# Turning rows by VectorE and DMA instead of TensorE in a four-layer block, and moving DMA issues from SyncE to ScalarE

## The chip, the cores and the metric

The kernel runs on one core of one Trainium2 chip. The metric is the device time of one launch in microseconds (us), as the median of several runs. The engines are named as in the profile: PE (TensorE, with its weight loads PEld), DVE (VectorE), ACT (ScalarE), POOL (GpSimd) and SP (SyncE, which only issues DMAs here). Each engine works through its own list of instructions in order and waits at semaphores for the others.

## The reference

Four layers follow each other on an input of 4 batches of 512 rows with 512 features, each with a layer norm in front and a residual sum behind:

```python
x = x + attn_a(layernorm(x), Wq, Wk, Wv, Wo)      # 16 heads, 4 key heads, width 128
x = x + ffn(layernorm(x), w1, w2, w3)              # ternary weights, width 1408
x = x + attn_b(layernorm(x), wq, wk, wv, wo, ...)  # 16 heads, block-scaled weights
x = x + ffn(layernorm(x), w1, w2, w3)              # the same weights again
```

Attention a is the mean of two: softmax attention of rotated queries and keys under a causal mask, and a gated linear attention, whose state decays at each row by `exp(log_sigmoid(k) / 16)`; there queries and keys are softmaxed over the 128 features instead of rotated. The feed-forward layer is `(sigmoid(x1) * x2) @ w3q.T` with `x1 = x @ w1q.T`, `x2 = x @ w2q.T` and weights rounded to -1, 0, 1.

## The kernel before, in words

All arithmetic of the main path is in 32-bit floats. Where the weights are exact in fewer bits, an operand is split into a high and a low half ("xnhi", "xnlo"), and two matmuls of a faster kind take the place of one. PE contracts over partitions, so rows have to be turned (transposed) before they are multiplied.

**Layer norm.** `layernorm_steps` (L123) gives the normalised rows of one batch in four chunks of 128. Each chunk takes statistics (L132, L133), a scale (L138 to L145), the normalised chunk `xn` (L160), four PE transposes of 128x128 into a bank of PSUM (L165), and the evacuation: a copy on ACT in attention, and in the feed-forward a split into halves by ACT and DVE (L120, L121). It is a generator: its user calls for the next part between other work.

**First attention** (`first_attention_gentle`). A group is one batch and one key head with its four query heads; there are 16 groups of four chunks, so 64 chunks. `Group` projects keys and values (L188 through `project`), makes the gates and the decays (`decays`): the running decay `down`, its value at each chunk's last row (`ends`, three small DMAs by SP, L420), its inverse `held`, the rotated keys `kr` (two DVE operations, L343 and L346, and two on POOL between them, L345), and the softmaxed, decayed keys `kd` (L358). `transposes` turns `kr` and `kd` by PE, four transposes each (L364); ACT evacuates them, with a factor 1/sqrt(128) for `krT` (L430). `states` (L439 to L443) follows.

`Chunk` has the parts A (project 128 query rows of four heads), B (softmaxed, decayed queries `qd` and rotated queries `qr`), L, C (PE turns `qr`), own (scores of the linear attention inside the chunk, L480), D(h) (for one head: scores by PE L490, mask and maximum by DVE L494, exponential by ACT L497, reciprocal L498, division by ACT L499, a turn of 32x32 blocks by DVE L500), E, F (L515 to L522: the product with the values) and G (the output projection and the residual sum, L193).

Queries `qd` and weights `pr` are turned without PE already: DVE turns 32x32 blocks, SP stores the tile to DRAM (`queries` L463, `passed` L503), and four DMAs of 32 partitions each read it back with the blocks in their places (L, L470, and E, L509).

**Order.** `step(n)` runs one part of several chunks: E and own for chunk n, D for n+1, C and L for n+2, A and B for n+3, F for n-1, G for n-2, and between them parts of the next group (`part(m, p, half)`: projections for p = 0 and 1, decays at p = 2, transposes at p = 3, states at p = 4), of a layer norm (`ln`) and of the quantisation of the feed-forward weights (`quant`, which loads a block by SP and takes its absolute sum by ACT, L233). For steps 0 to 63 PE's instructions stand in the order of the program (`manual_schedule`); on the other engines a scheduler places them when it expects their inputs, but instructions under `in_place` keep the program's order among themselves.

**Second feed-forward layer** (`feed_forward` with `last`). For each batch 11 blocks of 128 hidden features: two times eight matmuls (L188), then sigmoid on ACT (L1097), product on DVE (L1098), split into halves; then for each chunk of rows 22 matmuls and the residual sum (L1109), and the store of the output (L1111). The normalised rows of the next batch are made meanwhile by `halved`, one call behind each block from the third on (two behind the third).

Of the kernel before, what the change touches and what calls it, by code (L numbers as in the profile page):

```python
# [19 lines left out]
P = 128  # L20
# [54 lines left out]
def hybrid_block(ctx: ExitStack, tc: tile.TileContext, a: dict, out: bass.AP):  # L75
# [47 lines left out]
    def layernorm_steps(b, sink, tag="tp", apart=False, place=lambda i: i):  # L123

# [21 lines left out]

        if not apart:
            for c in range(NC):
                moments(c)
                if c == 1:  # L150
                    yield
            scales(slice(0, NC))
        for c in range(NC):
            if apart:
                moments(c)
                scales(slice(c, c + 1))
            else:
                yield
            xn = lnp.tile([P, C], F32, tag="xn", name="xn", bufs=1)
            nc.vector.tensor_scalar(xn, xs[b * NC + c], mv[:, c, 0:1], rstd[:, c : c + 1], ALU.subtract, ALU.mult)  # L160
            if not apart:
                yield
            tp = bank(tag, [P, NK, P])
            for k in range(NK):
                t = nc.tensor.transpose(tp[:, k, :], xn[:, k * P : (k + 1) * P], ident)  # L165
                if k == 0:
                    place(t)
            sink(c, tp)
# [5 lines left out]
    def halved(pool, b, **kw):  # L174

        halves = [pool.tile([P, NK, S], F32R, tag=f"xn{n}", name=f"xn{n}") for n in ("hi", "lo")]
        return halves, layernorm_steps(b, lambda c, tp: split(*(h[:, :, c * P : (c + 1) * P] for h in halves), tp), **kw)

# [132 lines left out]
    def first_attention_gentle(base, extra):  # L311
# [6 lines left out]
        with ExitStack() as st:  # L318
# [47 lines left out]

            xnTs = {}
# [6 lines left out]
            class Group:  # L374
# [32 lines left out]
                def decays(self):  # L407
# [11 lines left out]
                    for c in range(NC - 1):  # L419
                        nc.sync.dma_start(self.ends[:, c : c + 1], self.down[P - 1 : P, c, :])  # L420
# [6 lines left out]

                def transposes(self):
                    self.krT = two.tile([P, S], F32, tag="krT", name="krT")
                    transposed(self.krT.rearrange("p (c t) -> p c t", c=NC), self.kr, lambda o, i: nc.scalar.mul(o, i, SCALE))  # L430
                    self.kdT = two.tile([P, NC, P], F32, tag="kdT", name="kdT")
                    transposed(self.kdT, self.kd, nc.scalar.copy)
# [12 lines left out]
            class Chunk:  # L445
# [9 lines left out]
                def B(self):  # L455
                    c = self.c
                    qd = one.tile([P, HG, D], F32, tag="qd", name="qd")
                    softmax_decayed(qd, self.q_t, lambda h: self.k.down[:, c, :])

                    turned = one.tile([P, 4, HG, 32], F32, tag="turned", name="turned")  # L460
                    nc.vector.transpose(turned.rearrange("p q h t -> p h q t"), qd.rearrange("p h (q j) -> p h q j", q=4))
                    self.queries = dram.tile([P, HG * D], F32, tag="queries", name="queries", bufs=3)
                    in_place(nc.sync.dma_start(self.queries, turned.rearrange("p q h t -> p (q h t)")))  # L463
                    self.qr = two.tile([P, HG, D], F32, tag="qr", name="qr")
                    rotate(self.qr, self.q_t, turn[:, c : c + 1, 0:1, :], turn[:, c : c + 1, 1:3, :])

                def L(self):
                    qdT = two.tile([P, 4, HG, 32], F32, tag="qdT", name="qdT", bufs=4)
                    for q in range(4):
                        in_place(nc.sync.dma_start(qdT[32 * q : 32 * (q + 1)].rearrange("j a h t -> j a (h t)"), self.queries.rearrange("(a j) (q x) -> q j a x", a=4, q=4)[q]))  # L470
                    self.qdT = qdT.rearrange("p a h t -> p h a t")
# [12 lines left out]
                def D(self, h):  # L484
# [5 lines left out]
                    nc.tensor.matmul(sc.rearrange("p q (k j) -> p q k j", j=32), lhsT=self.qrT[:, h, :], rhs=self.k.krT.rearrange("p (k q j) -> p q k j", q=4, j=32)[:, :, :n, :], start=True, stop=True)  # L490
# [3 lines left out]
                    nc.vector.tensor_tensor_reduce(sc, sc, causal[:, :, 32 * (3 - c) :], -1.0, 3e38, ALU.add, ALU.min, nm)  # L494
# [6 lines left out]
                    if h == HG - 1:  # L501
                        self.passed = dram.tile([P, 4 * HG * P], F32, tag="passed", name="passed", bufs=3)[:, : 4 * HG * 32 * n]
                        in_place(nc.sync.dma_start(self.passed, self.turned))  # L503
# [48 lines left out]
            def step(n):  # L552
# [17 lines left out]
                if w:  # L570
                    w.E()
                part(m, p, 0)
                if n == -6:
# [4 lines left out]
                if x:  # L578
                    x.D(0)
                if z and n > -2:  # L580
# [4 lines left out]
                if x:  # L585
                    x.D(1)
                if p:
# [22 lines left out]
                if x:  # L610
                    x.D(3)
                if n in (-2, *range(NC + 1, last, NC)):
# [464 lines left out]
    def feed_forward(base, last, first):  # L1077

        with ExitStack() as st:
# [7 lines left out]
            for b in range(B):  # L1087
                ready, steps = halved(base, b + 1, place=in_place) if b + 1 < B else (None, iter(()))
                hid = []
                for f, (w, _) in enumerate(ws):  # L1090
# [11 lines left out]
                    for _ in range((f > 1) + (f == 2)):  # L1102
                        next(steps, None)
                    yield b, f
                for c in range(NC):
                    y = bank("mm", [P, C])
# [87 lines left out]
```

## Time and profile before

| what | us |
|---|---|
| median of 3 runs | 2468.93 (2465.59 to 2472.8) |
| profiled execution, its own time | 2466.74 |
| its span | 2464.8 |
| DVE busy | 1643.5 |
| ACT busy | 1210.8 |
| POOL busy | 387.6 |
| PE transposes of `kr` (L364), busy, 64 | 10.1 |
| PE transposes of `xn` (L165) in all layers, busy, 256 | 39.9 |
| SP's query stores (L463): issue, median to landing | 0.34, 2.8 |
| SP's row stores (L503): issue, median to landing | 0.34, 4.3 |
| SP's chunk-end decays (L420): issue, median to landing | 0.48, 4.5 |
| SP's query reads (L470): median to landing | 3.3 |

The page lists busy time as a union of intervals; PE's matmuls overlap, since one is started before the last has come out, and each 32-bit matmul has two records. DMA issues do not count as busy time. The first attention runs from the start to about 1010 us, the first feed-forward layer to about 1280, the second attention to about 2195, and the second feed-forward layer to the end.

### The profile page before, as it was taken

How to read it: one execution, taken by the hardware profiler on the slowest of the kernel's cores; microseconds unless marked ns; L12 is line 12 of the kernel's file. 1: busy time of each engine (PE TensorE's matmuls, PEld its weight loads, DVE VectorE, ACT ScalarE, POOL GpSimd, SP SyncE). 2: the span in 40 equal slices, each digit the busy share in tenths (PEclk: the TensorE clock that was granted, in tenths of full speed). 3: DMA queues.
4: the chain of work that ended last, by engine and by line, in shares of the span. 5: the costliest groups of instructions: out<-in, count | busy, mean ns of one | idle time of the engine just before them, and what ended most of it. 6: DMA issues, size and time to landing. Idle time of an engine off the chain costs nothing.

```text
span 2464.8 us, 28979 instructions
## 1 busy us (share of the span) xinstructions
PE 2425.2 (98%) x8552; PEld 1543.2 (63%) x8552; DVE 1643.5 (67%) x3816; ACT 1210.8 (49%) x3066; POOL 387.6 (16%) x424
## 2 busy tenths in 40 slices
PE   7999999999999999899999999999999999999998
PEld 4555555555555555488876666666666666658887
DVE  5888777878788888355558676667766666663332
ACT  5666666666666665333336455444444444432221
POOL 1222222222122222022224333100000000000000
PEclk9999999999999999999999999999999999999999
DMA  4667776777656664564536777534343435333000
GB/s 137 198 191 204 201 204 182 205 205 201 180 175 192 196 180 149 193 190 129 143 125 169 199 201 200 144 105 128 91 131 87 132 92 144 78 97 121 18 18 19
DMA packets 240616, 367.11 MB, mean 149 GB/s; under 512 B 41664, under 2 KB 126912, under 8 KB 234304
## 3 DMA queue, kind: packets, MB, share of 16 engines
q1 hardware_dynamic: 214192, 305.03, 44.2%
q10 hardware_dynamic: 18576, 34.95, 4.7%
q0 software_dynamic: 7680, 25.17, 3.6%
q8 instruction: 71, 1.16, 0.2%
q14 instruction: 97, 0.79, 0.1%
HBM read 209.53 MB, written 88.34 MB: 121 GB/s over the span
## 4 chain that ended last, share of the span: by engine, by line
PE 86%; DVE 5%; DMA 3%; issue 2%; ACT 1%; SPq 1%; POOL 1%; DVEq 0%; ACTq 0%; POOLq 0%
PE mm L188 44%; PE sc L188 10%; PE sc L890 8%; PE pv L520 5%; PE sc L490 5%; PE pv L924 4%; PE tp L924 4%; PE sc L480 2%; PE tp L364 2%; PE pv L518 1%; SPq L917 1%; DMA block<-blocks 1%; PE tp L165 1%; DMA prT<-turned 1%; DMA wo<-in_Wo 0%
## 5 line engine op out<-in xcount | busy, mean ns | idle before, releaser
L895 ACT ACTIVATE pr<-sc,nm 128x512 f32<-128x512 f32 x256 | 175.9, 687 | 301.6 <-DVE nm L892 258.3
L188 PE MATMUL sc<-xnhi,block 128*128 128x512 f32 x704 | 278.6, 396 | 3.7 <-ACT hT L1097 2.8
L188 PE MATMUL sc<-xnlo,block 128*128 128x512 f32 x704 | 275.4, 391 | 0.0
L890 PE MATMUL sc<-kT,qT 128*128 128x512 f32 x512 | 262.1, 594 | 0.4 <-ACT kT L872 0.4
L188 PE MATMUL mm<-xnhi,w 128*128 128x512 f32 x512 | 254.4, 497 | 0.0
L188 PE MATMUL mm<-wo,oT 128*128 128x512 f32 x512 | 232.2, 596 | 4.4 <-DMA wo<-in_Wo 3.8
L188 PE MATMUL mm<-wq,xnT 128*128 128x512 f32 x512 | 230.9, 594 | 0.1
L892 DVE TENSOR_REDUCE nm<-sc 128x1 f32<-128x512 f32 x256 | 174.9, 683 | 73.4 <-PE sc L890 70.9
L188 PE MATMUL mm<-xnlo,w 128*128 128x512 f32 x512 | 205.8, 402 | 0.0
L912 DVE STREAM_TRANSPOSE turned<-pr 128x512 f32<-128x512 f32 x256 | 173.4, 696 | 36.8 <-ACT pr L902 34.0
L499 ACT ACTIVATE pr<-pr,den 128x128 f32<-128x128 f32 (+3 forms) x256 | 141.5, 557 | 86.3 <-DVE den L498 84.5
L902 ACT ACTIVATE pr<-pr,den 128x512 f32<-128x512 f32 x192 | 138.2, 722 | 82.3 <-DVE den L900 82.1
L345 POOL TENSOR_TENSOR sw<-q_t,turn 128x256 f32<-128x256 f32 x128 | 97.1, 780 | 495.5 <-ACT q_t L453 396.5
L490 PE MATMUL sc<-krT,qrT 128*128 128x512 f32 (+3 forms) x512 | 170.4, 434 | 0.4 <-DVE own L482 0.4
L497 ACT ACTIVATE pr<-sc,nm 128x128 f32<-128x128 f32 (+3 forms) x256 | 132.9, 520 | 64.0 <-DVE nm L494 54.9
L188 PEld LDWEIGHTS mm<-wo,oT 128*128 128x128 f32 x512 | 96.3, 191 | 105.3 <-issue 95.0
L188 PEld LDWEIGHTS mm<-wq,xnT 128*128 128x128 f32 x512 | 96.3, 191 | 105.1 <-issue 98.8
L500 DVE STREAM_TRANSPOSE turned<-pr 128x128 f32<-128x128 f32 (+3 forms) x256 | 128.4, 503 | 46.7 <-ACT pr L499 43.4
L188 PEld LDWEIGHTS sc<-xnhi,block 128*128 128x128 f32 x704 | 132.8, 189 | 33.3 <-ACT hT L1097 4.0
L188 PEld LDWEIGHTS sc<-xnlo,block 128*128 128x128 f32 x704 | 132.8, 189 | 27.8 <-issue 0.7
L520 PE MATMUL pv<-prT,v_t 128*128 128x512 f32 x320 | 148.0, 592 | 0.0
L890 PEld LDWEIGHTS sc<-kT,qT 128*128 128x128 f32 x512 | 95.8, 189 | 81.4 <-issue 63.6
(151 smaller groups left out, 4800.7 us busy)
## 6 DMA issues: line engine op xcount, KB each, us to landing
prT<-turned SPq DMA_DIRECT2D x1024, 64.0 KB, 2.0
w<-exact SPq DMA_DIRECT2D x32, 1024.0 KB, 5.5
wq<-in_Wq ACTq DMA_DIRECT2D x16, 1024.0 KB, 5.3
queries<-turned SPq DMA_DIRECT2D x64, 256.0 KB, 2.8
qdT<-queries SPq DMA_DIRECT2D x256, 64.0 KB, 3.3
wo<-in_Wo ACTq DMA_DIRECT2D x16, 1024.0 KB, 6.1
passed<-turned SPq DMA_DIRECT2D x16, 1024.0 KB, 4.3
prT<-passed SPq DMA_DIRECT2D x64, 256.0 KB, 5.9
```

The costliest lines, as they stand in the source:

```text
L188: nc.tensor.matmul(acc, lhsT=lhs(k), rhs=rhs(k), start=k == 0, stop=k == n - 1)
L490: nc.tensor.matmul(sc.rearrange("p q (k j) -> p q k j", j=32), lhsT=self.qrT[:, h, :], rhs=self.k.krT.rearrange("p (k q j) -> p q k j", q= ...
L497: nc.scalar.activation(pr, flat, AF.Exp, bias=nm, scale=-1.0, accum_out=den)
L499: nc.scalar.mul(pr, pr, den)
L500: nc.vector.transpose(self.turned.rearrange("p (q h x) -> p q h x", q=4, h=HG)[:, :, h, :], pr.rearrange("p (q x) -> p q x", q=4))
L520: nc.tensor.matmul(acc.rearrange("p h (a t) -> p h a t", a=4), lhsT=self.k.v_t[:, j, :], rhs=self.wts[:, :, :, j, :], start=j == c == 0, s ...
L890: nc.tensor.matmul(sc, lhsT=qTs[u][:, i * P : (i + 1) * P], rhs=kTs[u], start=True, stop=True)
L892: nc.vector.tensor_reduce(nm, sc, AX.X, ALU.max, negate=True)
L895: nc.scalar.activation(pr, sc, AF.Exp, bias=nm, accum_out=den)
L902: nc.scalar.mul(pr, pr, den)
L912: nc.vector.transpose(turns[u][:, :, i, :], pr.rearrange("p (q k) -> p q k", q=4))
L924: nc.tensor.matmul(accs[u].rearrange("p (n t) -> p n t", t=32), lhsT=v_ts[m, j][:, h * D : (h + 1) * D], rhs=prTs[u].rearrange("p a i (k t ...
```

## The change

Three things change.

1. The rotated keys are turned like the queries: DVE turns 32x32 blocks (`turn_keys`, at p = 3 of the group), ACT stores them (`store_keys`), SP reads them back in four DMAs (`quarters`). The factor 1/sqrt(128) goes from the evacuation, which is gone, into the constant of the scores' mask and maximum.
2. The stores of queries and of weights are issued by ACT instead of SP, the query store at the end of the step (behind D(3)), the row store in the next step (behind D(0)) and the reads of the rows (E) behind D(1) instead of at the step's start. The three chunk-end decays of a group are issued by ACT.
3. In the second feed-forward layer the rows of batches 1 to 3 are turned by DVE, a store and four reads, both by SP (`halved_by_dma`); ACT and DVE make the halves from SBUF. Its parts are called behind every block and ahead of every chunk's output matmuls.

The PE order of the built program is otherwise the same; on DVE, ACT and SP the scheduler places instructions anew. The core of the diff:

```diff
+        def rows(c):
+            xn = lnp.tile([P, C], F32, tag="xn", name="xn", bufs=1)
+            nc.vector.tensor_scalar(xn, xs[b * NC + c], mv[:, c, 0:1], rstd[:, c : c + 1], ALU.subtract, ALU.mult)
+            return xn
...
+    def to_dram(turned, c, rows):
+        nc.vector.transpose(turned.rearrange("p q k i -> p k q i"), rows(c).rearrange("p (k q j) -> p k q j", k=NK, q=4))
+        passed = dram.tile([P, C], F32, tag="rows", name="rows", bufs=3)
+        in_place(nc.sync.dma_start(passed, turned.rearrange("p q k i -> p (q k i)")))
+        return passed
+
+    def from_dram(back, passed):
+        for q in range(4):
+            in_place(nc.sync.dma_start(back[32 * q : 32 * (q + 1)].rearrange("j (a x) -> j a x", a=4), passed.rearrange("(a j) (q x) -> q j a x", a=4, q=4)[q]))
+        return back.rearrange("p (a k i) -> p k a i", a=4, k=NK)
+
+    def in_halves(halves, c, back):
+        hi, lo = (h[:, :, c * P : (c + 1) * P].rearrange("p k (a i) -> p k a i", a=4) for h in halves)
+        in_place(nc.scalar.copy(hi, back))
+        nc.vector.tensor_tensor(lo, back, hi, ALU.subtract)
+
+    def halved_by_dma(pool, spare, b):
...
+        def steps():
+            moments, scales, rows = statistics(b)
+            for c in range(NC):
+                moments(c)
+            scales(slice(0, NC))
+            passed, backs = {}, {}
+            for c in range(NC + 2):
+                yield
+                if c < NC:
+                    passed[c] = to_dram(spare.tile([P, 4, NK, 32], F32, tag="turned", name="turned"), c, rows)
+                yield
+                if 0 < c <= NC:
+                    backs[c - 1] = from_dram(spare.tile([P, C], F32, tag="back", name="back"), passed[c - 1])
+                if c > 1:
+                    in_halves(halves, c - 2, backs[c - 2])
...
+            def turned_blocks(src):
+                turned = one.tile([P, 4, 4, 32], F32, tag="turned", name="turned")
+                nc.vector.transpose(turned.rearrange("p q n t -> p n q t"), src.rearrange("p n (q j) -> p n q j", q=4))
+                return turned
+
+            def to_dram_blocks(turned):
+                to = dram.tile([P, 4 * P], F32, tag="queries", name="queries", bufs=4)
+                in_place(nc.scalar.dma_start(to, turned.rearrange("p q n t -> p (q n t)")))
+                return to
...
                     for c in range(NC - 1):
-                        nc.sync.dma_start(self.ends[:, c : c + 1], self.down[P - 1 : P, c, :])
+                        in_place(nc.scalar.dma_start(self.ends[:, c : c + 1], self.down[P - 1 : P, c, :]))
...
+                def turn_keys(self):
+                    self.blocks = turned_blocks(self.kr)
+
+                def store_keys(self):
+                    self.keys = to_dram_blocks(self.blocks)
+
                 def transposes(self):
-                    self.krT = two.tile([P, S], F32, tag="krT", name="krT")
-                    transposed(self.krT.rearrange("p (c t) -> p c t", c=NC), self.kr, lambda o, i: nc.scalar.mul(o, i, SCALE))
+                    krT = two.tile([P, S], F32, tag="krT", name="krT")
+                    quarters(krT, self.keys)
+                    self.krT = krT.rearrange("p (q k j) -> p q k j", q=4, j=32)
...
-                    in_place(nc.sync.dma_start(self.queries, turned.rearrange("p q h t -> p (q h t)")))
+                    self.blocks = turned_blocks(qd)
...
+                def store_queries(self):
+                    self.queries = to_dram_blocks(self.blocks)
...
-                    if h == HG - 1:
-                        self.passed = dram.tile([P, 4 * HG * P], F32, tag="passed", name="passed", bufs=3)[:, : 4 * HG * 32 * n]
-                        in_place(nc.sync.dma_start(self.passed, self.turned))
+
+                def store_rows(self):
+                    self.passed = dram.tile([P, 4 * HG * P], F32, tag="passed", name="passed", bufs=3)[:, : 4 * HG * 32 * (self.c + 1)]
+                    in_place(nc.scalar.dma_start(self.passed, self.turned))
...
-                if w:
-                    w.E()
                 part(m, p, 0)
+                keys = groups[m] if p == 3 and 0 <= m < B * KV else None
+                if keys:
+                    keys.turn_keys()
...
                 if x:
                     x.D(0)
+                if w:
+                    w.store_rows()
...
                 if x:
                     x.D(1)
+                if keys:
+                    keys.store_keys()
+                if w:
+                    w.E()
...
                 if x:
                     x.D(3)
+                if z:
+                    z.store_queries()
...
-                    for _ in range((f > 1) + (f == 2)):
+                    for _ in range(1 if last else (f > 1) + (f == 2)):
                         next(steps, None)
                     yield b, f
                 for c in range(NC):
+                    next(steps, None)
```

## The prediction

> **What bounds the kernel now.** I read the page's busy times first, then the windows by stage, then what TensorE (PE) waits for, then single instructions in the timeline. Busy shares:
>
> ```profile
> span 2464.8 us, 28979 instructions
> PE 2425.2 (98%) x8552; PEld 1543.2 (63%) x8552; DVE 1643.5 (67%) x3816; ACT 1210.8 (49%) x3066; POOL 387.6 (16%) x424
> ```
>
> PE is idle for 39.6 us of the span in all. The windows (length, then busy time of PE, weight loads, DVE, ACT, POOL, the granted clock, DMA) show where: 0 to 62 us the start, 186 to 496 us the first attention in steady state, 2195 us to the end the second feed-forward layer.
>
> ```profile
> 0.00:62.00 62.00, 45.69 (x165) 30.95 (x166) 35.67 (x114) 33.44 (x108) 11.04 (x21) 0.92 0.48 138
> 186.00:496.00 310.00, 309.89 (x994) 170.54 (x993) 247.24 (x666) 197.87 (x606) 68.04 (x71) 1.00 0.70 199
> 2195.00:2465.00 270.00, 258.80 (x1144) 209.21 (x1142) 91.17 (x151) 61.82 (x103) 1.21 (x2) 0.99 0.14 50
> ```
>
> In steady state PE misses 0.11 us of 310, DVE is at 80% and ACT at 64%. So PE's own list of instructions sets the time there, and a PE instruction taken out pays what it holds PE for, as long as nobody else becomes late. The start is different: 16.3 us of 62 are idle, it is a chain of dependences.
>
> **What a transpose holds PE for.** The timeline in steady state, and in the second feed-forward layer (start, duration, instruction; rows of the other engines left out):
>
> ```profile
> 487.91 0.60 PE L364 MATMUL tp<-ident,kr 128*128 128x128 f32 x4
> 488.35 0.60 PE L364 MATMUL tp<-ident,kd 128*128 128x128 f32 x4
> 488.79 0.59 PE L188 MATMUL mm<-wo,oT 128*128 128x512 f32 x1
> ```
>
> ```profile
> 2291.14 0.39 PE L188 MATMUL sc<-xnlo,block 128*128 128x512 f32 x1
> 2291.37 0.60 PE L165 MATMUL tp<-ident,xn 128*128 128x128 f32 x4
> 2291.72 0.47 PE L188 MATMUL sc<-xnhi,block 128*128 128x512 f32 x1
> ```
>
> Durations overlap, so I take start to start: four transposes hold PE for 0.44 us in attention and 0.35 us in the feed-forward. The page's mean of one (283 ns for kr) would make four of them 1.13 us and is wrong for this purpose.
> The Trainium skill, "TensorE: Matmul & The Clock Gate", section "Part 4: PE-mode transpose", gives about 275 ns for a transpose in a kernel's context; by that the 112 transposes removed would be worth 30.8 us. The durations here agree with it, the distances between starts do not, and the sum goes by the starts.
>
> **The change, part by part.**
>
> (1) Keys' transposes of groups 1 to 15: 15 x 0.44 = **-6.6 us**. What replaces them lies on DVE (15 turns of 128x512; the row of the same operation for the queries has 0.67 us each, 10 us over 1000, on an engine with 20% idle) and on DMA queues: a store (queries' store row: 2.8 us to landing) and four reads (qdT row: 3.3 us). The turned keys are first used by the scores three steps (some 45 us) later, so the 7 us trip is covered; without that cover it would cost up to 7 us for each group. The scores' matmuls read keys in another order of the same 512 columns; I take nothing, since matmuls with strided and with plain moving operands both start 0.43 us apart. "VectorE: DVE Perf Modes", section "Rules for kernel authors", speaks against this edit: it gives a 128x128 transpose to TensorE where PSUM will do as destination. By engine time alone that is right here too (28 turns of 0.67 us on DVE for 28 groups of about 0.4 us on PE would lose 8 us), but only if DVE were the bound.
>
> (2) The rows of the second layer, batches 1 to 3: 12 x (0.35 + 0.01 for the slower matmul behind) = **-4.3 us**. A DVE turn, a store, four reads, and the same ACT and DVE halves take their place. DVE is busy for 91 of 270 us here and ACT for 62. Between a store and the reads lie three hidden blocks and between reads and use two, at 3.6 us each; both exceed the landing times of 2.8 and 3.3 us. All halves are made before the batch's output matmuls end. I see nothing late next.
>
> (3) ACT no longer copies krT (16 x 0.58 us), which frees a transpose bank sooner. PE waited for exactly this copy, 1.6 us at 67 us of the span; that wait goes, with about 0.3 us at 178 us where kr's and kd's transposes together waited: **-1.9 us**.
>
> (4) The start, group 0. Rows of before:
>
> ```profile
> 30.85 0.69 DVE L346 TENSOR_TENSOR kr<-kr,sw 128x512 f32<-128x512 f32 x1
> 31.62 1.57 POOL L345 TENSOR_TENSOR sw<-q_t,turn 128x256 f32<-128x256 f32 x2 [5.49 <-DVE kr L346]
> 32.26 1.60 DVE L358 SCALAR_TENSOR_TENSOR kd<-kd,den,held 128x128 f32<-128x128 f32 x4
> 34.61 0.72 POOL L345 TENSOR_TENSOR sw<-q_t,turn 128x256 f32<-128x256 f32 x1 [1.42 <-DVE qr L346]
> 34.94 0.63 PE L188 MATMUL mm<-wkv,xnT 128*128 128x256 f32 x1
> ```
>
> In the built order of the changed kernel DVE has, between the sum kr and the products kd: the turn of kr, a rotated query's sum, a maximum, and a second query's sum. The first sum waits for POOL (31.62 + 1.57 = 33.2) and ends at 33.9; POOL has one buffer for its products, so the second pair runs from 34.05 for 1.41 us to 35.5, and the second sum ends at 36.2. Only then kd begins, at 36.2 instead of 32.26. PE's queue holds kd's transposes and behind them the next group's projections, which begin near 38.1 instead of 34.94: **+3.1 us**, already without group 0's kr transposes. Nothing behind it on PE is free to run earlier. The bounds are 0 (later waits of the start take it up: PE still idles some 6 us between 50 and 68 us) and +3.9 (all of kd's delay). I take 3.1, as those later waits hang on the same projections.
>
> (5) Stores and decays moved from SP to ACT: 64 query stores, 64 row stores, 48 chunk-end decays; with the new 16 key stores 192 issues. The issue rows are 0.338 us for a store and 0.476 for a decay, 71.5 us in all, 4.5 for each group of 61 us. ACT runs in order, so an issue also makes everything behind it wait: behind the decays stands the exponential of held, then kd's exponentials; behind a row store q_t's copy; behind a query store often a weight block's absolute sum. Below: all hidden, and what PE still waits goes too (the windows from 62 to 990 us leave 3.1 us idle, 1.9 of them counted in part 3, so -1.2). Above: +71.5, if no issue lay beside other work. I take **+1.3**: in the timeline ACT's two weight loads (0.37 us each) are issued while the instruction before them runs, and ACT idles 36% here, waiting 1 to 3 us at a time for DVE without PE noticing. On SP the moves take waits away, which nobody on PE waited for.
>
> (6) Order. The row store moves from the end of a step on SP to behind the next step's first score on ACT, and the reads of the rows move from that step's start to behind its second score. In before SP came to one such store at 491.69, though its turn had ended by 485.4, so ACT is no later; the rows are used at the end of the following step, some 20 us behind the reads, for landings of 4.3 and 5.9 us. The query store moves from mid-step to the step's end; its reads come at the next step's start as before, and the use two steps later. Nothing for both; without the cover a step would wait up to 10 us. The factor 0.088 in the scores' maximum changes no instruction: nothing.
>
> Sum: -6.6 - 4.3 - 1.9 + 3.1 + 1.3 = **-8.4 us**. The profiled execution took 2466.74 us (span 2464.8 and 1.9 around it), so 2458.3; the median of the three runs shown is 2468.93, 2.2 above, so 2460.5, and I say 2460.
>
> **Rivals.**
>
> *Given back, within 0.3%.* kd's transposes now follow the own-chunk scores directly, 0.44 us earlier, and kd is later by the decays' issues (3 x 0.476). In a quiet group kd ends at 483.39 + 1.14 = 484.5 for use at 488.35, a cover of 3.8 us: nothing. In the four groups with a layer norm beside them the cover was already gone once (the 0.3 us above). At 1.5 us for each of these and 0.2 for the others that is 6.0 + 2.4 = 8.4 us less 1.3 counted: a net of -1.3, about 2468. For it: DVE at 80%. Against: 0.11 us of waiting in 310.
>
> *Slower: ACT stands at a DMA's semaphore.* Each DMA carries one of a few semaphores and first waits for that one's previous owner, whatever it carried. The trace shows it on SP:
>
> ```profile
> SPq L420 <- DMA wq<-in_Wq: 41.5, 5, 8.7
> SPq L503 <- DVE turned L500: 131.6, 31, 7.4
> SPq L463 <- DVE turned L461: 149.3, 49, 7.3
> ```
>
> The decays waited five times for a weight load that they don't need, 41.5 us in total, 8.7 at longest. On ACT such a wait stands between down and held. The cover is the 3.8 us above: five waits beyond it give 41.5 - 19 = 22.5 us, 2483 in all; from 1.7 us beyond the cover at five places the whole gain is lost. Against: in the built order most of the decays' owners are row stores and queries of about 7 us of ACT's work earlier, and those land in 4.3 us; the stores' own waits for DVE come where the turn is mostly done.
>
> *The rows alone pay.* Keys gain nothing, for any of the reasons above: -4.3 + 3.1 to -4.3, 2465 to 2468; it counts with the first rival.
>
> **How the numbers follow.** A difference under about 0.3% (7.4 us) can't be told from none by a measurement of this kernel. Forecast 0.50 (faster, 2453 to 2461.5; the lower end is the start's delay taken up and part 5 at its lower bound, 2460.5 - 3.1 - 2.5 = 2454.9, and 2 us for the scatter of the runs, which lie 7.2 us apart); given back 0.33 (same); slower 0.17, nearly all above 2476. The range: 2453 to 2476; it leaves out the slower case and a little below.
>
> **What would show it.** Right: the kr and the 48 xn rows gone, PE busy by about 11 us less, groups of four steps 0.44 us shorter, the window of the second layer 4.3 us shorter, projections of group 1 near 38 us. Wrong: PE's list of waits with kd, q_t or the scores' banks behind ACT in steady state; an ACT wait that ends with a DMA; idle PE in 62 to 990 us above some 5 us.

## The result and the profile after

The changed kernel takes 2502.74 us (median of 6 runs, 2496.45 to 2507.24), the kernel before 2469.25 us beside it (6 runs, 2465.59 to 2472.8): a ratio of 1.0136, 95% interval 1.0119 to 1.0153. It is slower by 33.5 us where 8 us of gain were predicted, and lies above the range. The two executions that were profiled, 2466.74 and 2505.87 us, lie 39 us apart, so a few us between two profiles are not yet a difference of the kernels. Line numbers from here on are those of the kernel that a row comes from; in the changed kernel the projections are L239, the decays' copy `held` L482, the row store L576, and all four turnings' line L421.

The page of the changed kernel:

```profile
span 2504.1 us, 28859 instructions
PE 2429.3 (97%) x8440; PEld 1535.8 (61%) x8440; DVE 1642.0 (66%) x3844; ACT 1207.4 (48%) x3050; POOL 379.4 (15%) x424
```

112 instructions are gone from TensorE (PE), 8552 to 8440, and yet it is busy for longer, 2429.3 us against 2425.2. Its idle time rose from 39.6 to 74.8 us. The same three windows (the last moved by the 40 us that come before it; columns as in the prediction):

```profile
0.00:62.00 62.00, 42.31 (x146) 28.50 (x147) 33.10 (x102) 29.54 (x96) 9.74 (x19) 0.86 0.43 132
186.00:496.00 310.00, 302.26 (x955) 164.07 (x954) 235.56 (x650) 191.61 (x585) 62.94 (x69) 1.00 0.70 203
2236.00:2504.00 268.00, 256.61 (x1103) 206.47 (x1102) 100.36 (x166) 62.09 (x103) 2.01 (x2) 0.99 0.22 75
```

The steady window, which missed 0.11 us of 310 before, now misses 7.74, and that is where the loss is. By the starts of TensorE's instructions:

| stretch | before, us | after, us | difference | predicted |
|---|---|---|---|---|
| start to the first own-chunk scores | 60.4 | 63.9 | +3.5 | +3.1 |
| from there to the last own-chunk scores | 949.3 | 989.4 | +40.1 | -7.2 |
| from there to the end of the first feed-forward layer | 273.4 | 273.7 | +0.2 | 0 |
| second attention, to its last rows | 925.1 | 927.1 | +1.9 | 0 |
| second feed-forward layer to its last block | 248.8 | 243.4 | -5.3 | -4.3 |
| tail | 7.8 | 6.6 | -1.2 | 0 |

The start came out as worked out: kd's products run at 35.59 (36.2 predicted, 32.26 before) and the next projections at 38.33 (38.1).

```profile
35.59 1.13 DVE L409 SCALAR_TENSOR_TENSOR kd<-kd,den,held 128x128 f32<-128x128 f32 x4
38.33 1.91 PE L239 MATMUL mm<-wkv,xnT 128*128 128x256 f32 x4
```

What TensorE waits for in the changed kernel (us in total, times, longest):

```profile
PE mm L239 <- DVE held L482: 15.1, 11, 2.3
...
PE mm L239 <- DMA wo<-in_Wo: 8.6, 2, 6.7
...
PE mm L239 <- ACT gatehi L120: 4.3, 4, 1.6
PE mm L239 <- DVE state L516: 4.2, 6, 1.5
PE mm L239 <- DVE gatelo L121: 4.0, 4, 1.4
```

The first row doesn't occur in before at all, and the second is 3.8 us there (the last group's load took 8.5 us to land, 5.3 in before). The first: a product waits, in 11 groups, for VectorE's copy of the decays. One such place, before (TensorE's last decays product, the output projection behind it, VectorE's copy):

```profile
535.93 0.40 PE L188 MATMUL mm<-gatelo,until 128*128 128x512 f32 x1
536.16 3.60 PE L188 MATMUL mm<-wo,oT 128*128 128x512 f32 x8
539.61 0.67 DVE L415 TENSOR_SCALAR held<-mm 128x512 f32<-128x512 f32 x1
```

and after, with ScalarE's row store and the copy of the queries ahead of it:

```profile
552.92 0.33 ACTq L576 DMA_DIRECT2D passed<-turned  x1
553.35 0.59 ACT L527 COPY q_t<-mm 128x512 f32<-128x512 f32 x1 [0.91 <-DVE low L301]
554.46 0.40 PE L239 MATMUL mm<-gatelo,until 128*128 128x512 f32 x1
555.29 0.68 DVE L482 TENSOR_SCALAR held<-mm 128x512 f32<-128x512 f32 x1
556.02 3.27 PE L239 MATMUL mm<-wo,oT 128*128 128x512 f32 x7 [1.17 <-DVE held L482]
```

Before, the output projection starts right behind the decays, 3.45 us before VectorE copies them. After, it starts when that copy is done, though no value of the decays goes into it. What ties them is a PSUM bank. Projections, decays and states share two banks under one name (`mm`). In the built program of before the two are used strictly in turn all through the first attention. In that of the changed kernel the turn is broken 19 times there, and in 11 of the 14 groups where an output projection follows the decays, it was given the bank that the decays have just filled, not that of the queries. The source doesn't say so anywhere: it asks for a bank of that name, and which one is decided when the order is built.

VectorE too waits for something new, in 15 places: to turn a block into a buffer that a store has not yet read.

```profile
DVE turned L421 <- DMA queries<-turned: 19.1, 15, 2.8
```

### The profile page after: what moved, and what is told of

Same layout as the page of the kernel before. It is cut to its first block, busy times and chain, and to the rows that moved or that the text cites. A ratio compares the mean times of both kernels' runs of the same rounds, so it can differ in the third digit from the quotient of the medians.

```text
span 2504.1 us, 28859 instructions
## 1 busy us (share of the span) xinstructions
PE 2429.3 (97%) x8440; PEld 1535.8 (61%) x8440; DVE 1642.0 (66%) x3844; ACT 1207.4 (48%) x3050; POOL 379.4 (15%) x424
## 4 chain that ended last, share of the span: by engine, by line
PE 80%; DVE 8%; DMA 4%; issue 3%; ACT 2%; SPq 1%; POOL 1%; ACTq 0%; DVEq 0%; POOLq 0%
PE mm L239 41%; PE sc L239 9%; PE sc L972 8%; PE tp L1006 4%; PE pv L1006 4%; PE sc L562 4%; PE pv L593 4%; PE sc L552 1%; PE pv L591 1%; DMA queries<-turned 1%; PE tp L415 1%; DVE sc L566 1%; SPq L999 1%; DMA block<-blocks 1%; DMA wo<-in_Wo 1%
## 5 line engine op out<-in xcount | busy, mean ns | idle before, releaser
L239 PE MATMUL sc<-xnhi,block 128*128 128x512 f32 x704 | 277.7, 395 | 4.1 <-ACT hT L1184 2.8
L239 PE MATMUL sc<-xnlo,block 128*128 128x512 f32 x704 | 275.1, 391 | 0.0
L239 PE MATMUL mm<-wo,oT 128*128 128x512 f32 x512 | 240.3, 614 | 24.3 <-DVE held L482 15.1
L239 PE MATMUL mm<-xnhi,w 128*128 128x512 f32 x512 | 254.4, 497 | 0.0
L239 PE MATMUL mm<-wq,xnT 128*128 128x512 f32 x512 | 232.8, 598 | 4.3 <-DVE state L516 4.2
L239 PE MATMUL mm<-xnlo,w 128*128 128x512 f32 x512 | 205.8, 402 | 0.0
L239 PEld LDWEIGHTS mm<-wo,oT 128*128 128x128 f32 x512 | 98.0, 196 | 132.7 <-issue 99.1
L239 PEld LDWEIGHTS mm<-wq,xnT 128*128 128x128 f32 x512 | 96.4, 192 | 112.0 <-issue 99.9
L239 PEld LDWEIGHTS sc<-xnhi,block 128*128 128x128 f32 x704 | 132.8, 189 | 34.0 <-ACT hT L1184 4.0
L239 PEld LDWEIGHTS sc<-xnlo,block 128*128 128x128 f32 x704 | 132.8, 189 | 27.9 <-issue 0.7
```

Of the source, the lines that this page charges most:

```text
L239: nc.tensor.matmul(acc, lhsT=lhs(k), rhs=rhs(k), start=k == 0, stop=k == n - 1)
```

## The theories

Theory 1: the banks out of turn bring the loss. Theory 2: the issues themselves, 71.5 us of ScalarE's time, hold its other work wherever they stand. Theory 3: the keys' way through DRAM. Theories 4 to 6 came up on the way: the place of the row stores in ScalarE's order (4), one buffer for two turnings (5), SyncE held by a key store (6).

## Experiments

Times are medians. Behind each stands its ratio to the kernel before, measured beside it at 2469.14 to 2470.43 us, with the 95% interval. Edits are to the kernel named.

### The parts by themselves

**Feed-forward rows alone.** Before, with `halved_by_dma` and its steps as in the change. The score products of the first attention read the keys' columns in plain order here, not by quarters, and so they do in the run of the issues alone further down: these two kernels do the same work on the same shapes, but their scores are not the attention's.

> The kernel before with the second feed-forward layer's rows of batches 1 to 3 by VectorE and DMA, and nothing else. All theories: the stretch from the last rows of the second attention to the last block of this layer took 248.76 us before and 243.41 us in the changed kernel, its tail 7.8 and 6.6 us, so this part alone should give -5 to -6.5 us: 2462 to 2465 us. If it gives nothing (2468 or more), what looked like its gain came from somewhere else.

Measured: 2461.86 us, ratio 0.9969 (0.9956 to 0.9981). With the keys' columns read in the order of before:

> As the run with the feed-forward rows alone, whose score products read the keys' columns in plain order; here they read them in the order of the kernel before. All theories: 2461 to 2464 us, as there.

Measured: 2463.47 us, 0.9965 (0.9952 to 0.9977). This part gives 6.2 to 7.5 us and is the only one that pays.

**The issues on ScalarE alone**, without the keys and the feed-forward rows:

> The kernel before with the query stores, row stores and decays issued by ScalarE at their new places, keys still transposed by TensorE, feed-forward as before. Theory 1, banks: with the issues on ScalarE the built order gives the output projection the PSUM bank of the decays in some 11 groups of 16, so that it waits for VectorE's copy of the decays (held); the loss is all here: 2469 + 35 to 45 = 2504 to 2515 us. Theory 2, ScalarE's issues in order hold its other work: the same range. Theory 3, the keys' way through DRAM (VectorE's turning, a later key bank) is what costs: 2465 to 2473 us here, and no wait of the output projection for held.

Measured: 2502.53 us, 1.0127 (1.0110 to 1.0144), +33.2 us, with the wait for held in 11 places again. Theory 3 falls as the main cause: without any key in DRAM the whole loss is there. (The three kinds of issue by themselves, below, read the keys by quarters and come to the same sum.)

**Banks in turn in the changed kernel, out of turn in before.**

```diff
-    def bank(tag, shape):
+    def bank(tag, shape, turns=itertools.cycle(("mm0", "mm1"))):
+        tag = next(turns) if tag == "mm" and "mm0" in ps[1] else tag
...
-    with banks(mm=2, sc=3, tp=2, pv=1)
+    with banks(mm0=1, mm1=1, sc=3, tp=2, pv=1)
```

> The changed kernel with one thing altered: its two PSUM banks of the projections, decays and states are used strictly in turn, as they are in every one of 516 uses in the kernel before; TensorE's order stays the same but for a few instructions at the start. Theory 1, banks: the waits of the output projection for held (16.9 us over 11 groups) and of the query projection for the states (5.5 us) go: 2502.7 - 22 to 45 = 2458 to 2481 us. Theory 2, ScalarE's issues hold its other work: the waits only change their name: 2495 to 2505 us. Theory 3, keys' way: 2495 to 2505 us.

Measured: 2492.87 us, 1.0095 (1.0079 to 1.0112). 9.9 us come back and the wait for held is gone, but the time lies between the two ranges: the banks are part of the loss and not all of it. The query projection's waits for the states did not go: 7.3 us in 7 places, against 4.2 in 6 in the list above (which has 15.1 us for held, not the 16.9 that the expectation names). The converse, in before, by the same two tags, with the output projection of the decays' step not taking its turn:

```diff
+        if tag in ("mm", "same") and "mm0" in ps[1]: turn[0] ^= tag == "mm"; tag = f"mm{turn[0]}"
...
-        lambda h: self.k.wo[:, h, :], HG)
+        lambda h: self.k.wo[:, h, :], HG, "same" if self.c == 1 and self.k.b * KV + self.k.g < B * KV - 2 else "mm")
```

> The kernel before with one thing altered: in 14 groups the output projection of the decays' step takes the bank that the decays have just filled, and not the other one; no store, issue or transpose is moved. Theory 1, banks: the output projection waits for held once in each of 14 groups, 1.5 us each by the 11 places of the changed kernel (16.9 us), and what follows from it: 2469 + 18 to 45 = 2487 to 2514 us. Theories 2 and 3: 2466 to 2473 us, since nothing that they blame is here.

Measured: 2544.57 us, 1.0301 (1.0273 to 1.0328): +75 us, far above the range, because in before VectorE comes to the decays' copy 3.5 us after TensorE, so that each wait is longer than the 1.5 us I had taken over from the changed kernel:

```profile
PE mm L188 <- DVE held L415: 50.1, 15, 4.7
```

So a bank out of turn costs time by itself, without any moved store, and the more the later VectorE comes to the copy.

**Each kind of issue by itself**, in before:

```diff
+                def store_rows(self):
+                    self.passed = dram.tile(...)
+                    in_place(nc.scalar.dma_start(self.passed, self.turned))
...
                 if x:
                     x.D(0)
+                if w:
+                    w.store_rows()
```

(and `w.E()` behind `x.D(1)`, as in the change)

> The kernel before with only the 64 row stores issued by ScalarE at their new place (between the first two scores of the next step) and the loads of these rows moved behind them; queries' stores, decays and keys as before. Theory 4, the place of the row store: on ScalarE it waits for VectorE's last turning of the rows, and the copy of the queries stands behind it; this alone brings nearly all of the loss of the issues (33.2 us): 2495 to 2505 us, with the output projection waiting for held. Theory 2, the issues' time: 64 of 176 issues bring their share, 2478 to 2483 us.

Measured: 2497.36 us, 1.0111 (1.0094 to 1.0128): **+27.5 us**.

```profile
PE mm L188 <- DVE held L415: 17.0, 13, 2.3
```

The query stores at the step's end on ScalarE:

> The kernel before with only the 64 query stores issued by ScalarE at the end of the step. Theory 4: they stand behind work that has long ended, so 2466 to 2473 us. Theory 2, the issues' time: their share of 33.2 us, 2478 to 2483 us.

Measured: 2474.87 us, 1.0022 (1.0013 to 1.0032): +5.0 us, between the two ranges. The decays on ScalarE:

> The kernel before with only the 48 decays at the chunks' ends issued by ScalarE, between the two exponentials of a group. Theory 4: 2467 to 2473 us; the 1.4 us of three issues per group end before the kd that they delay is needed. Theory 2, the issues' time: 48 issues of 0.476 us, 2475 to 2481 us.

Measured: 2471.66 us, 1.0006 (0.9994 to 1.0017): +1.8 us, not told from none. 27.5 + 5.0 + 1.8 = 34.3, against 33.2 for the three together: the parts add up, and by far the most is the row stores'. 64 row stores take as long to issue as 64 query stores, so it isn't issue time (theory 2). The reverse, in the changed kernel, with row stores and their loads back on SyncE:

> The changed kernel with only the row stores and the loads behind them put back on SyncE at their old places; queries' and keys' stores and decays stay with ScalarE. Theory 4, the place of the row store: the loss goes, 2502.7 - 33 to 45 = 2457 to 2470 us. Theory 2: two thirds of the issues stay, 2485 to 2495 us. Theory 3, keys' way: 2485 us or more, since it is all still there.

Measured: 2480.01 us, 1.0038 (1.0023 to 1.0052): 22.7 us come back, and no wait for held is left. The time lies between the ranges of theories 4 and 2, 10 us above theory 4's; the section on the keys finds these 10 us.

### The place of the row store

In the run of before with row stores on ScalarE, the store moved one score down:

```diff
-                if w:
-                    w.store_rows()
...
                 if w:
+                    w.store_rows()
                     w.E()
```

> As the run with only the row stores on ScalarE, but each store stands one score later, directly ahead of the loads that read it, and so behind the copy of the queries on ScalarE. Theory 4, the place: the copy of the queries no longer stands behind a wait for VectorE's last turning, the two banks go in turn again, and of the 27.5 us that the row stores brought 0 to 8 are left: 2468 to 2478 us. Rival, the row stores cost on ScalarE wherever they stand (issue time, or their rows read later): 2490 us or more.

Measured: 2477.16 us, 1.0027 (1.0016 to 1.0037). Of 27.5 us 6.7 are left; no output projection has the decays' bank, and none waits for held. With the store at the first place and the banks in turn:

> As the run with only the row stores on ScalarE at the first place, with the two banks used strictly in turn. It divides the 27.5 us: if the bank is all of it, 2469 to 2475 us; if ScalarE's wait ahead of the queries' copy is all, 2495 to 2500 us. From the changed kernel, where the turns gave 10 of 33 us back, some 2484 to 2490 us.

Measured: 2480.52 us, 1.0038 (1.0026 to 1.0051), better than I had put it: 17.4 of the 27.5 us are the banks', 10.1 the rest. A part of the rest, in this run and in the one before it, is the last group's load of the output weights: in all seven kernels with row stores on ScalarE TensorE waits 6.0 to 7.3 us for it at longest, in before and the others 3.4 to 3.9. Why it lands later there was not tested. That the bank depends on the place is shown by the two programs. Why, I infer: at the first place the store is held by VectorE's last turning, and the copy of the queries, which frees the other bank, stands behind it, so whoever hands out banks while the order is built finds the decays' bank free earlier.

### The keys

With row stores on SyncE and the rest of the change kept (2480.01 us), parts alone would give 2469.9 - 7 + 5.0 + 1.8 = 2469.7 without the keys. The keys cost 10 us there, where 5 were to be gained by the prediction's steps. That kernel's waits of VectorE and TensorE:

```profile
DVE turned L421 <- DMA queries<-turned: 29.2, 12, 4.2
```

```profile
PE mm L239 <- DVE state L516: 11.2, 8, 2.5
```

The keys' turning takes the one buffer (`turned`, one copy) that the queries' turning uses. It waits until the query store has read it, and the decayed states, which stand behind it on VectorE, come late for the query projection, whose bank they hold. With the keys turned into the buffer of the plain keys, which nobody reads any more:

```diff
-                    self.blocks = turned_blocks(self.kr)
+                    self.blocks = turned_blocks(self.kr, "k_t")
```

> As the changed kernel with its row stores back on SyncE (2480.0 us), and the keys turned into a buffer that no query uses: that of the plain keys, which are read no more by then. Theory 5: VectorE's turning of the keys doesn't wait, the query projection's waits for the states (11.2 us in 8 places, with slow matmuls behind them) go: 2462 to 2472 us. If the keys' cost lies elsewhere: 2477 to 2483 us.

Measured: 2469.24 us, 0.9993 (0.9980 to 1.0005): 10.8 us come back, and the wait for the states with them. But this is level with 2469.7, so the keys still gain nothing. With everything on SyncE:

> The kernel before with only the keys' way through DRAM, every store and decay issued by SyncE. The prediction's steps for the keys (-6.6 - 1.9 + 3.1): 2462 to 2467 us. Theory 5, one buffer for two turnings: VectorE's turning of the keys waits until the store of the queries has read the same buffer (28 us in 11 places in the kernel with row stores back on SyncE), and the decayed states stand behind it: 2472 to 2482 us.

Measured: 2477.79 us, 1.0031 (1.0021 to 1.0041). The range of theory 5, but not its mechanism: TensorE waits 0.7 us in all for the states here. In the profile 6.4 us are the start (first own scores at 66.8 us), but not by the prediction's chain: with the decays on SyncE kd's products run at 32.38 us, as in before, though VectorE turns the keys ahead of them. In the run above with the decays alone on ScalarE, where VectorE turns no key, they run at 36.69 us, and the first own scores at 65.1. All seven kernels with the decays on ScalarE have these scores at 63.9 to 67.2 us, all others at 59.3 to 60.6, but for this run and one more. So the prediction's +3.1 us belongs to the decays' move. kd's products here, and with the decays alone:

```profile
32.38 1.67 DVE L409 SCALAR_TENSOR_TENSOR kd<-kd,den,held 128x128 f32<-128x128 f32 x4
```

```profile
36.69 1.13 DVE L358 SCALAR_TENSOR_TENSOR kd<-kd,den,held 128x128 f32<-128x128 f32 x4
```

What is late in this start is ScalarE, which waits 5.86 us for a block of feed-forward weights:

```profile
54.02 0.74 ACT L284 ACTIVATE w<-w 128x640 f32<-128x640 f32 x1 [5.86 <-DMA w<-in_w1T]
```

SyncE issued that load at 47.42 us, behind ScalarE's 1 MB load of the output weights at 47.04; in before it went out first, at 44.00 against 46.02. The profile of the rows alone with the keys in the order of before, where TensorE turns all keys, has the same wait (6.46 us, the loads at 45.62 and 44.95) and its first own scores at 65.3 us. So this loss also occurs without any key in DRAM. Group 0's keys left to TensorE:

```diff
+                    if self.b == self.g == 0:
+                        transposed(self.krT.rearrange("p q k j -> p k q j"), self.kr, ...)
+                    else:
+                        quarters(krT, self.keys)
```

> The kernel before with only the keys of groups 1 to 15 through DRAM, those of group 0 transposed by TensorE, everything issued by SyncE. If the start (own scores at 66.8 us in place of 60.4) is the loss of the keys alone: 2477.8 - 6.4 = 2471 us, and less by the 6.6 us of the prediction's step if the steady groups gain: 2462 to 2472 us. If the loss lies in the steady groups: 2474 to 2480 us.

Measured: 2473.38 us, 1.0012 (1.0001 to 1.0023), between the two ranges. The profile has the first own scores at 59.8 us, but it is of one of the two fastest of ten executions (2465.84 and 2466.13 us; the others take 2472.27 to 2476.86), so it doesn't say how the others started. With the feed-forward rows added:

> The kernel before with the feed-forward rows by VectorE and DMA and the keys of groups 1 to 15 through DRAM, those of group 0 transposed by TensorE; all stores and decays by SyncE. If the start is what eats the keys' gain: 2461.9 - 6 = 2454 to 2458 us. If 15 groups without the keys' transposes give nothing: 2460 to 2466 us.

Measured: 2466.23 us, 0.9989 (0.9976 to 1.0002), 2.8 us above the rows alone. How much of the keys' loss is the start stays open, but 15 groups without transposes gain nothing: from the first own-chunk scores to the last the profile has 953.8 us here, and 953.3 and 953.7 us in the two runs of the rows alone. The load of the output weights tells where it goes; its row (DMA issues, median us to landing) in before, and with the keys of groups 1 to 15 in DRAM:

```profile
wo<-in_Wo ACTq DMA_DIRECT2D x16, 1024.0 KB, 6.1
```

```profile
wo<-in_Wo ACTq DMA_DIRECT2D x16, 1024.0 KB, 8.8
```

```profile
PE mm L239 <- DMA wo<-in_Wo: 9.1, 9, 3.7
```

In before this load lands 2.2 to 3.2 us ahead of its use in 13 steady groups. Here SyncE is late in the step with the key store, and the row loads of the next step go out beside the load (at 325.04 us against a load issued at 327.49; in before at 318.44 against 329.16); it takes up to 10.2 us, and the output projection waits for it in nine places, in before in two. My reading was that SyncE stands for the turned keys (theory 6), so I took the key store off SyncE, and nothing else:

> Feed-forward rows by VectorE and DMA, keys of groups 1 to 15 through DRAM, query and row stores and decays by SyncE as before; only the 15 key stores by ScalarE. Theory 6, SyncE held by the key store: it stands for the turned keys, the row loads behind it go out 6 us later and meet the load of the output weights. Without that wait this load takes 6.1 us again, the output projection waits for it in the last two groups alone, and the keys' gain shows: 2455 to 2460 us. If the keys gain nothing for another reason: 2462 to 2468 us.

Measured: 2495.54 us, 1.0098 (1.0080 to 1.0116), 29 us above the run with that store on SyncE, where 6 to 11 of gain were expected. The load is back at 6.2 us, but the time went elsewhere. One group (TensorE, VectorE, ScalarE's issue):

```profile
320.55 0.67 DVE L421 STREAM_TRANSPOSE turned<-kr 128x512 f32<-128x512 f32 x1
321.25 0.34 ACTq L426 DMA_DIRECT2D queries<-turned  x1
323.38 0.71 DVE L421 STREAM_TRANSPOSE turned<-qd 128x512 f32<-128x512 f32 x1 [2.16 <-DMA queries<-turned]
...
326.51 2.85 PE L239 MATMUL mm<-wq,xnT 128*128 128x512 f32 x3 [2.31 <-DVE state L519]
```

The queries' turning stands 2.16 us for the key store, the sums of the states behind it, and TensorE behind them, in 12 groups:

```profile
PE mm L239 <- DVE state L519: 25.2, 12, 3.2
```

That is the shared buffer from the other side. With this in mind I went back to the run with the key store on SyncE. There the two turnings and SyncE's wait read:

```profile
309.27 0.67 DVE L421 STREAM_TRANSPOSE turned<-kr 128x512 f32<-128x512 f32 x1
...
316.49 0.67 DVE L421 STREAM_TRANSPOSE turned<-qd 128x512 f32<-128x512 f32 x1
```

```profile
SPq L426 <- DVE turned L421: 5.1, 1, 5.1
```

The queries were turned at 310.32 us in before; here they stand behind the keys' turn and store, 6.2 us later, and SyncE waits 5.1 us for them, not for the keys. So theory 6 had the collision right and its cause wrong; the order of these rows points to theory 5's buffer again, though a run with this store on SyncE and a second buffer was not made. With the store on ScalarE and a buffer of the keys' own besides:

> As the run before, with the keys turned into the buffer of the plain keys. Theory 5 (one buffer for two turnings) has 0 to -3 us left here, since the query stores go out early by SyncE: 2453 to 2460 us; no change to the run before if the buffer matters only where ScalarE stores the queries late.

Measured: 2470.96 us, 1.0005 (0.9993 to 1.0018). 24.6 us are gone with the shared buffer, and the load of the output weights takes 6.1 us in most groups, but the time stays above its range: now the own-chunk scores wait for ScalarE in 7 places of the first attention (5.6 us). In no arrangement did the keys gain.

**The change with its causes mended** (row store one score later, a buffer for the keys, group 0 on TensorE):

> The changed kernel with three causes mended and everything else kept, its 176 issues on ScalarE too: row stores directly ahead of their loads, keys turned into a buffer of their own, group 0's keys by TensorE. By the parts measured alone: 2469.9 - 7.5 (rows) + 6.7 (row stores there) + 5.0 (query stores) + 1.8 (decays) and 0 to -6 for the keys: 2468 to 2477 us. If something else in the changed kernel costs: 2485 us or more.

Measured: 2486.42 us, 1.0056 (1.0039 to 1.0072). 16 of 33 us come back, 10 less than the parts let expect. The profile shows waits for the gates in four places (7.2 us), of the own-chunk scores for ScalarE in eight (3.7 us), and slow products behind them (last section); which edit brings these together was not separated, and stays open. The fastest kernel of all these is before with the feed-forward rows alone, 2461.86 and 2463.47 us.

## Why the prediction was wrong

**The step that failed is part 5 with part 6:** "I take **+1.3**" for the moved stores and decays, and "Nothing for both" for the order of the row and query stores. The same moves measure +33.2 us: row stores 27.5, query stores 5.0, decays 1.8 by themselves (the last not told from none). I had named the very instruction ("behind a row store q_t's copy") and then priced only its delay, for which ACT has room. What I didn't ask is what q_t's copy releases: one of two PSUM banks. With the copy behind the store in the built order, the output projection got the other bank, and with it a wait for VectorE that no source line shows. Banks in turn take 17.4 of the row stores' 27.5 us away, a place one score later 20.8; in the changed kernel as a whole banks in turn give 9.9 of 33.5 us back, row stores on SyncE 22.7. Why the query stores cost 5.0 us was not followed up.

Part 1, -6.6 us: the mechanism held, the sum didn't. In a quiet group the step with the keys' transposes takes 17.66 us where it took 18.10, which is the 0.44 predicted. But I covered the new trip to DRAM by the 45 us until its use, and it was not late there: it was late for others. Its turning shares one buffer with the queries', and through it VectorE, SyncE and the states are late, and the load of the output weights, 2.2 to 3.2 us early in before, was next. Keys alone measure +3.7 to +7.4 us by SyncE, in the larger figure with the order of two loads at the start, which comes without them too.

Part 2, -4.3 us: right in kind, too small in size. The layer takes 248.6 to 248.9 us in all profiles without this part and 242.8 to 243.4 in all with it, 5.2 to 6.1 us less; alone the part gives 6.2 to 7.5 us. The tail is not its gain: it is 6.5 to 6.7 us in seven kernels without the part too (7.8 in before). Why the layer gains more than the distances between the transposes' starts is open.

Part 3, -1.9 us: the wait for the krT copy is gone from the list, but at the same place, 69.5 us, TensorE now waits 2.7 us for VectorE's own-chunk product.

Part 4, +3.1 us: measured +3.5, by the chain given, since the prediction read it from the built order. But that order comes with the decays on ScalarE: there three issues stand between down and held, POOL's products for the second query begin behind held (after 0.87 us of waiting, with and without the keys' turn), and kd's products follow both query sums. With the decays on SyncE kd isn't late. So this term is a price of part 5, and the keys by the prediction's own steps were to gain 8.5 us.

Of the rivals, "ACT stands at a DMA's semaphore" had the right sign and the wrong issue: it put 22.5 us on the decays, which cost 1.8. The list of what would show it wrong named q_t's and the scores' banks behind ACT and idle PE above 5 us; the idle time came, by the same kind of bank, but behind VectorE.

## What to carry to other kernels

Before moving an instruction in the order of a busy engine, ask what it releases, not only how long it takes: compare the built programs' buffer and PSUM bank assignments, because a pool that hands out buffers by a planned order can turn a harmless move into a wait between two tiles that have nothing in common. A buffer with one copy ties its two users by the slowest reader, here a store's DMA; give a new user its own. And where one engine is busy all the time, a wait of 2 us can cost nearly 4, as the next section shows.

## What the runs showed of the hardware

Some waits cost more than they last. In the changed kernel TensorE waits 1.57 and then 1.32 us at 618 and 620 us, and the output projection behind it runs at half its rate:

```profile
620.48 5.29 PE L239 MATMUL mm<-wo,oT 128*128 128x512 f32 x8
```

Eight products took 3.60 us at 536.16 in before. Some of these start up to 854 ns apart where 429 is usual, 1.7 us more in all. The windows before and during it show the granted clock (last but two of the columns):

```profile
600.00:616.00 16.00, 16.00 (x50) 8.47 (x49) 14.44 (x40) 10.88 (x31) 2.41 (x3) 1.00 0.69 199
620.00:625.00 5.00, 4.86 (x8) 2.22 (x9) 4.59 (x13) 1.57 (x5) 2.09 (x3) 0.66 0.73 182
```

In the steady groups of the changed kernel single waits of 0.8 to 1.5 us left the distances alone; of those of 1.86 to 2.3 us some did and some were followed by 1.8 us of loss. The Trainium skill, "TensorE: Matmul & The Clock Gate", section "What's actually happening", has the clock fall to half after an idle window of about 3.4 us. The length of the slow stretch, about four products of 854 ns, agrees with such a window; its condition doesn't, since a single wait of 1.87 us sufficed here:

```profile
814.36 5.40 PE L239 MATMUL mm<-wo,oT 128*128 128x512 f32 x8 [1.87 <-DVE held L482]
```

```profile
815.00:820.00 5.00, 5.00 (x9) 2.01 (x8) 2.21 (x6) 4.49 (x20) 1.41 (x2) 0.66 0.98 242
```

This is part of why 13 waits of 17.0 us in all (row stores) cost 27.5 us, where two of the 13 were followed by such a stretch, and why 12 of 25.2 us (key stores on ScalarE) cost 29, with nine of them.
